# Logit columns of an attention layer turned by VectorE instead of TensorE, and the last half of the output summed by TensorE in PSUM

## The chip, the cores and the metric

The kernel runs on one core of a Trainium2 chip. The metric is the device time of one execution in microseconds (us), the median of several runs. Of the core's engines four compute: PE (TensorE, matrix products into PSUM; its weight loads are shown as PEld), DVE (VectorE), ACT (ScalarE) and POOL (GpSimd). SP (SyncE) only issues transfers. Each engine runs its own instructions in the order in which they were emitted, and waits for other engines and for transfers by semaphores.

## The reference

There are 16 batches of N = 1024 nodes with D = 128 values each, and one symmetric 0/1 matrix `adj` of 1024 x 1024 with ones on its diagonal. All is fp32.

```python
h = x @ Wo;  u1 = h @ a1;  u2 = h @ a2           # layer 0: attention
e = u1[:, idx1] + u2[:, idx2]                    # pair logits, a 1024 x 1024 matrix
e = where(e >= 0, e, 0.1 * e)
att = softmax(where(adj > 0, e, -9e15), axis=1)
x = layernorm(x + att @ h + x @ Ws)
h = x                                            # layer 1: five gated steps
for _ in range(5):
    m = adj @ h;  av = concat([m, m])
    g = h @ u3.T + b_u3
    z = sigmoid(av @ w3.T + b3 + g);  r = sigmoid(av @ w4.T + b4 + g)
    hv = tanh(av @ w5.T + b5 + (r * h) @ u5.T + b_u5)
    h = (1 - z) * h + z * hv
out = layernorm(x + h)
```

Because of how `idx1` and `idx2` run, the logit of row i and column j is, in the first 512 rows, (u1 + u2) of node 2i or 2i + 1, by the half of the columns that j lies in; in the last 512 rows it is u1[2j] + u2[2j + 1] (modulo 1024), the same for all rows. The softmax runs over the rows. So a batch needs three columns of 1024 numbers: u1, u2, and the exponential of the clipped leaky ReLU of u1 + u2.

## The kernel before

**The plan.** Every operation of the whole kernel, is put into a `Plan` (L53 on): engine, expected length in ns, a rank, a function that emits it, the tiles that it reads and writes, and a lag until its result is taken as seen. `order` (L79) plays this through like a clockwork: whenever an engine is free, it takes the ready operation of the lowest rank for which tile buffers are free. The order of starts found that way is the order in which the program is emitted. So nothing is written out by hand; lengths, lags and ranks set the order on every queue. Ranks come from a table `D` (one entry per kind of operation), a due time per batch and step (`rank_of` L321, `rank0` L324; 10 units from one pair of batches to the next), and `NUDGE`, small amounts added for single batches and steps. An `add` under the engine "DMA" emits nothing: it only tells the plan when a load is expected to land (`lands` L366).

**The start.** `early_loads` (L348) issues the first loads on SP's and ACT's queues: x of batch 0 in two halves, the row of attention weights, `Wo`, the halves of `adj`. `late_loads` (L376) issues the step weights, u3, u5 and five rows of biases in one block. PE meanwhile runs fillers: two products of `fill_` and 48 operations `idle_` of two transposes each (L439), of rank 9000, which are taken when nothing else is ready. `ahead` (L466) computes x(Ws + 1) for four later batches and puts it to DRAM. `own_weights` (L489) turns the biases into columns and adds the two halves of w3, w4, w5, since both halves of av are m.

**Layer 0**, `layer0(b)` (L654), for each batch: products ph (L686) give h and the two logit numbers of each node; hx (L696) takes them out of PSUM; `u_` (L701) and `p_` (L709) put three columns of 8 numbers per partition into `u`: two logit columns and an exponential. These must get from node-in-partition order into two other forms: `pb`, the exponentials of all nodes in every partition, and `uu`, pairs of logits in another arrangement of nodes. For batches 2 to 15 PE transposes u, 128 x 24, into PSUM (L725), DVE copies it (L730), SP stores it to `ud` in DRAM (L735), and loads it again as a broadcast (`pb`, L742) and, with two transfers of single numbers, as `uu` (L750). Batches 0 and 1 do without DRAM: 0 has its spreading products from the weights (L763), 1 multiplies each column by the unit matrix (L795) and ACT copies (L804); both have pair products of 4 columns (L813). Then come `t_` (L829: the sum `seen`, leaky ReLU), `q_`, the sums over neighbours `z_` (L849), the factor rz, the blocks hi (L901, ACT) and lo (L907, DVE), products `po` (L644), and a layernorm.

**Layer 1** works on pairs of batches, whose five steps interleave with those of the pair before and with layer 0 of later batches. `messages` (L1089) computes adj @ h by products of halves with seven instead of eight products per batch, using sums of quarters of adj (`sums_of_adj`, L512); operands pass through DRAM (X, loaded as G) where they must be turned. Steps listed as plain multiply directly (blocks `blk_h`, hi on ACT L632 and lo on DVE L636). `gates` (L1211), per half e of 512 nodes: pu (L1228), gate products (L1238), tanh for r and z (L1241), r times h (L1248), products for hv (L1254, L1255), tanh (L1260), and three DVE operations: less (L1263), times (L1266) and h (L1269). With tanh(x/2) in place of the sigmoid, h + 0.5 (z + 1)(hv - h) is the new h. Even batches keep h with the other sign.

**The end.** `end` (L1284), for the last two batches: x is loaded again from `yd` (L1291), h is transposed by PE (L594), DVE adds both (L1301), and `layernorm` (L535) takes statistics (DVE L540, L542), a power (POOL L546, L547) and scales (ACT L561, or for the very last half DVE L567, "short"). The output leaves on SP and ACT (L1318, L1320). The last step is 4, the last half (b, s, e) = (15, 4, 1).

## Time and profile before

| | us |
|---|---|
| median of 3 runs (lowest, highest) | 1450.19 (1449.73, 1451.22) |
| profiled execution | 1449.74 |
| its span, first to last instruction | 1447.6 |
| PE, DVE, ACT, POOL busy in the span | 1432.1, 1161.1, 895.3, 196.9 |

The mean granted clock of PE was 0.997; 1.00 in each stretch of the first 100 us, and 0.81 in the last 22.6 us, where PE is idle in the end. Transfers move 120 GB/s on average, and 340 GB/s in the first 25 us.

A group's row gives the line, engine, operation, output and inputs, how many, busy time and the mean of one in ns, then the idle time before it and what ended it. The timeline's rows give start, length, engine, line and operation; instructions of one line that follow each other are put together (x16), and square brackets give an idle time and its releaser. The queue of SP is SPq. Two matmul rows overlap, since a row holds the latency of a product and the next starts before it has ended: what a product costs a busy PE is the distance of two starts.

### The profile page before, as it was taken

How to read it: one execution, taken by the hardware profiler on the slowest of the kernel's cores; microseconds unless marked ns; L12 is line 12 of the kernel's file. 1: busy time of each engine (PE TensorE's matmuls, PEld its weight loads, DVE VectorE, ACT ScalarE, POOL GpSimd, SP SyncE). 2: the span in 40 equal slices, each digit the busy share in tenths (PEclk: the TensorE clock that was granted, in tenths of full speed). 3: DMA queues.
4: the chain of work that ended last, by engine and by line, in shares of the span. 5: the costliest groups of instructions: out<-in, count | busy, mean ns of one | idle time of the engine just before them, and what ended most of it. 6: DMA issues, size and time to landing. Idle time of an engine off the chain costs nothing.

```text
span 1447.6 us, 17700 instructions
## 1 busy us (share of the span) xinstructions
PE 1432.1 (99%) x4995; PEld 898.2 (62%) x4995; DVE 1161.1 (80%) x2748; ACT 895.3 (62%) x1790; POOL 196.9 (14%) x327
## 2 busy tenths in 40 slices
PE   9999999999999999999999999999999999999996
PEld 7666656666666666656566665666666665656563
DVE  6897888979888899968888788887987977764635
ACT  5666555666665666666746667567574676563644
POOL 1231000022111120111201011011110122000302
PEclk9999999999999999999999999999999999999998
DMA  8235234573335643454343643456424364222111
GB/s 280 96 105 180 61 94 131 153 211 110 108 105 146 188 111 109 122 163 117 102 124 111 189 104 93 116 161 175 107 77 109 96 203 124 80 59 68 50 44 31
DMA packets 187902, 174.14 MB, mean 120 GB/s; under 512 B 34238, under 2 KB 137236, under 8 KB 187796
## 3 DMA queue, kind: packets, MB, share of 16 engines
q1 hardware_dynamic: 181490, 154.71, 37.7%
q0 software_dynamic: 5888, 17.83, 3.7%
q8 instruction: 41, 0.67, 0.2%
q14 instruction: 65, 0.53, 0.1%
q10 hardware_dynamic: 418, 0.39, 0.1%
HBM read 95.61 MB, written 77.24 MB: 119 GB/s over the span
## 4 chain that ended last, share of the span: by engine, by line
PE 95%; DVE 2%; POOL 1%; DMA 0%; ACT 0%; issue 0%; SPq 0%; POOLq 0%; DVEq 0%; ACTq 0%
PE ps_acc_a L644 17%; PE ps_g_r L1238 9%; PE gz L1238 9%; PE ps_g_v L1254 9%; PE ps_g_v L1255 9%; PE ps_g_r L1228 9%; PE ps_acc_c L644 9%; PE ps_acc_po L644 7%; PE ps_acc L644 6%; PE gz L644 4%; PE ps_g_ph L686 2%; PE ps_idle L441 1%; PE ps_acc_po L978 1%; PE ps_t L594 1%; PE ps_acc_px L964 1%; PE ps_ahead L477 0%
## 5 line engine op out<-in xcount | busy, mean ns | idle before, releaser
L1254 PE MATMUL ps_g_v<-m,wm 128*128 128x512 f32 x320 | 163.5, 592 | 0.0
L1255 PE MATMUL ps_g_v<-r,u5h 128*128 128x512 f32 x320 | 163.4, 592 | 0.0
L1238 PE MATMUL ps_g_r<-m,wm 128*128 128x512 f32 x320 | 159.8, 593 | 0.1
L1238 PE MATMUL gz<-m,wm 128*128 128x512 f32 x320 | 159.4, 592 | 0.0
L1248 DVE SCALAR_TENSOR_TENSOR r<-r,hT 128x512 f32<-128x512 f32 x160 | 109.2, 687 | 61.9 <-ACT r L1241 60.6
L1263 DVE TENSOR_TENSOR hv<-hv,hT 128x512 f32<-128x512 f32 x160 | 109.6, 685 | 59.2 <-ACT hv L1260 58.4
L1228 PE MATMUL ps_g_r<-hT,u 128*128 128x512 f32 x320 | 154.2, 592 | 0.0
L644 PE MATMUL ps_acc_a<-tab,blk_s 128*128 128x512 f32 x544 | 150.4, 418 | 0.0
L1241 ACT ACTIVATE r<-ps_g_r,bh 128x512 f32<-128x512 f32 x160 | 109.6, 686 | 65.0 <-PE ps_g_r L1238 62.0
L644 PE MATMUL ps_acc_po<-adj,blk 128*128 128x512 f32 x512 | 143.7, 425 | 0.0
L1231 ACT COPY gz<-ps_g_r 128x512 f32<-128x512 f32 x160 | 91.1, 572 | 63.0 <-PE ps_g_r L1228 61.6
L644 PEld LDWEIGHTS ps_acc_a<-tab,blk_s 128*128 128x128 f32 x544 | 101.1, 188 | 36.3 <-issue 10.3
L1241 ACT ACTIVATE z<-gz,bh 128x512 f32<-128x512 f32 x160 | 109.7, 687 | 15.4 <-PE gz L1238 15.2
L644 PEld LDWEIGHTS ps_acc_po<-adj,blk 128*128 128x128 f32 x512 | 95.9, 188 | 37.1 <-issue 15.3
L1269 DVE SCALAR_TENSOR_TENSOR hT<-hv,hT 128x512 f32<-128x512 f32 x160 | 108.5, 679 | 2.3
L1266 DVE SCALAR_TENSOR_TENSOR hv<-z,hv 128x512 f32<-128x512 f32 x160 | 108.8, 680 | 0.8
L1255 PEld LDWEIGHTS ps_g_v<-r,u5h 128*128 128x128 f32 x320 | 60.7, 190 | 76.6 <-issue 62.0
L1238 PEld LDWEIGHTS gz<-m,wm 128*128 128x128 f32 x320 | 60.7, 190 | 73.9 <-issue 73.2
L644 PE MATMUL ps_acc<-adj,blk_h 128*128 128x512 f32 x384 | 100.8, 413 | 0.5 <-DVE us L730 0.5
L636 DVE TENSOR_TENSOR blk_s<-G,blk_s 128x512 fp32r<-128x512 f32 x136 | 91.8, 682 | 11.3 <-ACT blk_s L632 10.8
L602 DVE STREAM_TRANSPOSE T<-hT 128x512 f32<-128x512 f32 x138 | 96.2, 702 | 0.8 <-DMA D_y<-T_y 0.2
L1254 PEld LDWEIGHTS ps_g_v<-m,wm 128*128 128x128 f32 x320 | 60.3, 190 | 56.4 <-issue 48.9
(193 smaller groups left out, 2518.2 us busy)
## 6 DMA issues: line engine op xcount, KB each, us to landing
G<-X SPq DMA_DIRECT2D x140, 256.0 KB
X<-T SPq DMA_DIRECT2D x552, 64.0 KB
yd<-y POOLq DMA_DIRECT2D x32, 256.0 KB, 3.3
D_y<-T_y SPq DMA_DIRECT2D x112, 64.0 KB
F_y<-D_y SPq DMA_DIRECT2D x28, 256.0 KB
X<-y SPq DMA_DIRECT2D x28, 256.0 KB
D_b<-T_b SPq DMA_DIRECT2D x112, 64.0 KB
F_b<-D_b SPq DMA_DIRECT2D x28, 256.0 KB
```

Source lines behind the costliest of these rows:

```text
L602: nc.vector.transpose(T(t).rearrange("p (b c i) -> p b c i", b=4, c=4), turned(src()))
L636: lambda: nc.vector.tensor_tensor(half(1), src(), half(0), ALU.subtract),
L644: nc.tensor.matmul(T(bank), T(blk)[:, k, c, :], right(c), start=(first and i == 0), stop=(last and i == len(terms) - 1), skip_group_check= ...
L1228: nc.tensor.matmul(T(pr), u3, h(), start=True, stop=True)
L1238: nc.tensor.matmul(T(p_), wm[:, j, :], T(m), start=False, stop=True, skip_group_check=True)
L1241: nc.scalar.activation(T(t), T(p_), AF.Tanh, bias=bh[:, j : j + 1], scale=0.5 * sg)
L1248: lambda r=r, h=h: nc.vector.scalar_tensor_tensor(T(r), T(r), 1.0, h(), ALU.add, ALU.mult),
L1254: nc.tensor.matmul(T(pv), wm[:, 2, :], T(m), start=True, stop=False)
L1255: nc.tensor.matmul(T(pv), u5h, T(r), start=False, stop=True)
L1263: nc.vector.tensor_tensor(T(hv), T(hv), h(), ALU.subtract)
L1266: nc.vector.scalar_tensor_tensor(T(hv), T(z), 1.0, T(hv), ALU.add, ALU.mult)
L1269: nc.vector.scalar_tensor_tensor(h(), T(hv), 0.5, h(), ALU.mult, ALU.add)
```

## The change

1. **Attention row.** It is loaded first on ACT's queue, ahead of half of x.
2. **Logit columns.** `u` gets four columns instead of three (the first is the last column of h, which nothing reads), so that it is 128 x 32. DVE transposes it in blocks of 32 x 32 within SBUF; SP stores the result to `ud` as 128 rows of 32 numbers. PE's transpose and DVE's copy from PSUM go. Batch 1 takes this way too: its spreading and pair products and ACT's copies go, and it waits for transfers through DRAM.
3. **Transfers of the start.** The planned landings are set anew; `late_loads` become single operations that the plan puts behind batch 1's `uu` load (key `b1`), and so do the x loads from batch 4 on and those of the last batch of `ahead`. `layer0(1)` is planned ahead of the rest.
4. **The very last half.** A new function `finish` replaces less, times, h, transposes and addition of (15, 4, 1). The hv products and tanh come in two pieces of 256 columns. With old = (z - 1) h, PE sums x, -0.5 old and 0.5 (z + 1) hv, each against a unit matrix (turning the last two), into two PSUM banks, from which the layernorm reads. The epsilon of its variance is added by DVE. All of batch 15 is now scaled by DVE, and batch 14's last scale by ACT waits for the last tanh.
5. **Ranks.** `D` and `NUDGE` are set anew; `NUDGE` has new kinds of keys for halves and for operations of the end.

```diff
-NUDGE = {(3, 2): -0.6, (3, 3): 0.75, (0, 1): -0.45,
...
+NUDGE = {(3, 2): 1.8, (3, 3): 0.95, (0, 1): 0.15,
...
+(15, 4, 0): 0.15, (15, 2): 0.3, ('add', 14, 1): 0.15, ('add', 15, 0): -0.1, ('ln', 14, 1): -0.6, ('ln', 15, 0): -1.2, 15: 0.05, ('add', 14, 0): -0.6}
...
-        D = dict(m=-0.05, pu=1.4, u=0.95, pr=0.75, pz=0.85, r=0.45, pv=1.05, z=1.3, hv=0.5, h=1.2, tr=2.35, o=6.35, ln=2.5, out=4.4, l1=-9, l2=-7, l3=-2.2, l4=-4.5, l5=-7.25)
...
+        D = dict(m=-0.05, pu=-0.1, u=3.45, pr=0.75, pz=0.85, r=1.45, pv=0.05, z=2.8, hv=0.5, h=-0.8, tr=2.35, o=6.35, ln=2.5, out=4.4, l1=-9.2, l2=-9, l3=-2.2, l4=-3.5, l5=-7.25)
...
         def early_loads():
             nc.sync.dma_start(T(x0)[:, HALF:N], x_t[0][:, HALF:N])
+            nc.scalar.dma_start(T(ws)[0:1, P : 3 * P], att_w.rearrange("k o -> o k"))
             nc.scalar.dma_start(T(x0)[:, 0:HALF], x_t[0][:, 0:HALF])
-            nc.scalar.dma_start(T(ws)[0:1, P : 3 * P], att_w.rearrange("k o -> o k"))
...
-        lands(4650, [(x0, 0), (x0, 1), (ws, "att")])
-        lands(650, [(("wo",), 0)])
-        for ns, k, e in ((2000, 0, 0), (1400, 0, 1), (1400, 1, 0), (1400, 1, 1), (1600, 2, 0), (1400, 2, 1), (1400, 3, 0), (1400, 3, 1)):
+        lands(4700, [(x0, 0), (x0, 1), (ws, "att"), (("wo",), 0)])
+        for ns, k, e in ((1500, 0, 1), (3100, 0, 0), (300, 1, 1), (1900, 1, 0), (1800, 2, 1), (1000, 2, 0), (1700, 3, 1), (1500, 3, 0)):
...
-        lands(1400, [(("xt", 1), 0), (("xt", 1), 1)])
...
+        lands(500, [(("xt", 1), 0), (("xt", 1), 1)])
         def late_loads():
+            def load(t, what, to, by):
+                sp(450, -7.9, lambda: nc.sync.dma_start(to(), by), reads=[(("b1",), 0)], writes=[(t, what)], lag=2600)
             for j, w in enumerate((w3_t, w4_t, w5_t)):
-                nc.sync.dma_start(
...
+                load(
...
                 )
-            nc.sync.dma_start(u3, u3_t)
-            nc.sync.dma_start(u5, u5_t)
+            load(("uw",), 0, lambda: u3, u3_t)
+            load(("uw",), 1, lambda: u5, u5_t)
             for j, v in enumerate((w3_b, w4_b, w5_b, u3_b, u5_b)):
-                nc.sync.dma_start(T(ws)[j : j + 1, 3 * P : 4 * P], v.rearrange("(o p) -> o p", o=1))
...
+                load(ws, ("b", j), lambda j=j: T(ws)[j : j + 1, 3 * P : 4 * P], v.rearrange("(o p) -> o p", o=1))
...
-                    sp(450, -91, lambda x=x, b=b, hs=hs: nc.sync.dma_start(T(x), x_t[b][:, hs]), writes=[(x, "sent")], lag=0)
+                    sp(450, -91, lambda x=x, b=b, hs=hs: nc.sync.dma_start(T(x), x_t[b][:, hs]), reads=[(("b1",), 0)] if b == AHEAD[-1] else [], writes=[(x, "sent")], lag=0)
...
+            if split:
+                def half(i):
+                    for j in range(2 * i, 2 * i + 2):
+                        nc.vector.bn_stats(T(stats)[:, j, :], src(j))
+                    for j in range(2 * i, 2 * i + 2):
+                        nc.vector.bn_aggr(T(mv)[:, j, :], T(stats)[:, j, :])
+                    if i:
+                        nc.vector.tensor_scalar(T(rstd)[:, 0, :], T(mv)[:, :, 1], EPS, None, ALU.add)
+                dve(570, rank, lambda: half(0), reads=after[0:1], writes=[(stats, 0), (mv, "a")])
+                dve(730, rank, lambda: half(1), reads=[*after[1:2], (mv, "a")], writes=[(stats, 1), (mv, 0), (rstd, "e")])
...
-                sp(450, rank, lambda: nc.sync.dma_start(T(xt), x_t[b]), writes=[(xt, 0), (xt, 1)], lag=3500)
+                sp(450, rank, lambda: nc.sync.dma_start(T(xt), x_t[b]), reads=[(("b1",), 0)], writes=[(xt, 0), (xt, 1)], lag=3500)
...
-                nc.vector.tensor_copy(w[:, 0:2, :], h[:, :, P : P + 2].rearrange("p c t -> p t c"))
+                nc.vector.tensor_copy(w[:, 0:3, :], h[:, :, P - 1 : P + 2].rearrange("p c t -> p t c"))
...
-            if b >= 2:
-                put = ("ps", "t", b, "u")
-                pe(
-                    120,
+            if b >= 1:
+                dve(
+                    110,
                     rank,
-                    lambda: nc.tensor.transpose(T(put)[0 : 3 * NC, 0:P], T(u).rearrange("p t c -> p (t c)"), ident),
-                    reads=[(u, 0), (u, 1), (("ident",), 0)],
-                    writes=[(put, 0)],
-                )
-                dve(
-                    280, rank, lambda: nc.vector.tensor_copy(T(us), T(put)[0 : 3 * NC, 0:P]), reads=[(put, 0)], writes=[(us, 0)]
+                    lambda: nc.vector.transpose(T(us), T(u).rearrange("p t c -> p (t c)")),
+                    reads=[(u, 0), (u, 1)],
+                    writes=[(us, 0)],
                 )
                 sp(
                     450,
                     rank,
-                    lambda: nc.sync.dma_start(T(ud).rearrange("t (c p) -> (t c) p", p=P), T(us)),
+                    lambda: nc.sync.dma_start(T(ud).rearrange("t (c k i) -> k (t c) i", k=4, i=32), T(us)),
                     reads=[(us, 0)],
                     writes=[(ud, 0)],
                 )
                 sp(
                     450,
                     rank,
-                    lambda: nc.sync.dma_start(T(pb), T(ud)[2:3, :].to_broadcast([P, N])),
+                    lambda: nc.sync.dma_start(T(pb), T(ud)[3:4, :].to_broadcast([P, N])),
                     reads=[(ud, 0)],
                     writes=[(pb, 0), (pb, 1)],
                     lag=3000,
...
                 def uu_():
                     for w in range(2):
-                        nc.sync.dma_start(T(uu)[:, w, :], T(ud)[w].rearrange("(c p two) -> two p c", p=P, two=2)[w])
-                sp(950, rank, uu_, reads=[(ud, 0)], writes=[(uu, 0)], lag=3000)
+                        nc.sync.dma_start(T(uu)[:, w, :], T(ud)[w + 1].rearrange("(c p two) -> two p c", p=P, two=2)[w])
+                sp(950, rank, uu_, reads=[(ud, 0)], writes=[(uu, 0), *([(("b1",), 0)] if b == 1 else [])], lag=3000)
...
-                        def spread_(e=e, pp=pp):
-                            for j in range(4):
-                                c = 4 * e + j
-                                nc.tensor.matmul(
-                                    T(pp)[:, j * P : (j + 1) * P],
-                                    T(u)[:, 2, c : c + 1].to_broadcast([P, P]),
-                                    ident,
-                                    start=True,
-                                    stop=True,
-                                )
-                        def pb_(e=e, pp=pp):
-                            nc.scalar.copy(T(pb)[:, e * HALF : (e + 1) * HALF], T(pp))
-                        pe(920, rank, spread_, reads=[(u, 0), (u, 1), (("ident",), 0)], writes=[(pp, 0)])
-                        act(A, rank, pb_, reads=[(pp, 0)], writes=[(pb, e)])
...
+        def finish(b, s, rank, sg, m, r, z, hv, pv, h):
+            old, units = ("T", b, s, "old"), ("look", "units")
+            o, yd = ("y0", b, "o", 1), ("yd", b, 1)
+            plus, minus = T(units)[:, 0:P], T(units)[:, P : 2 * P]
+            def units_():
+                nc.vector.tensor_scalar(plus, ident, 0.5, None, ALU.mult)
+                nc.vector.tensor_scalar(minus, ident, -0.5, None, ALU.mult)
+            def old_():
+                nc.vector.scalar_tensor_tensor(T(old), T(z), 1.0, h(), ALU.subtract, ALU.mult)
+            dve(260, rank - 0.6, units_, reads=[(("ident",), 0), (m, 0)], writes=[(units, 0)])
+            sp(
+                450,
+                rank,
+                lambda: nc.sync.dma_start(T(o).rearrange("p c d -> p (c d)"), T(yd)),
+                reads=[(yd, 0), (("m", b, s, 0), 0)],
+                writes=[(o, "y")],
+                lag=2300,
+            )
+            dve(V, rank + D["hv"] - 0.3 + NUDGE.get(("old", b), 0), old_, reads=[(z, 1), (("hT", b), 1)], writes=[(old, 0)])
+            for f in range(2):
+                cs = slice(2 * P * f, 2 * P * (f + 1))
+                t = ("ps", "t", b, s, 1, f)
+                def pv_(cs=cs):
+                    nc.tensor.matmul(T(pv)[:, cs], wm[:, 2, :], T(m)[:, cs], start=True, stop=False)
+                    nc.tensor.matmul(T(pv)[:, cs], u5h, T(r)[:, cs], start=False, stop=True)
+                def hv_(cs=cs):
+                    nc.scalar.activation(T(hv)[:, cs], T(pv)[:, cs], AF.Tanh, bias=b5 if sg > 0 else nb5, scale=1.0)
+                def times_(cs=cs):
+                    nc.vector.scalar_tensor_tensor(T(hv)[:, cs], T(z)[:, cs], 1.0, T(hv)[:, cs], ALU.add, ALU.mult)
+                def y_(t=t, f=f):
+                    for j in range(2):
+                        nc.tensor.matmul(
+                            T(t)[:, j * P : (j + 1) * P], ident, T(o)[:, 2 * f + j, :], start=j == 0, stop=False, skip_group_check=True
+                        )
+                def add_(t=t, f=f, what=None, unit=None, last=False):
+                    for j in range(2):
+                        c = 2 * f + j
+                        nc.tensor.matmul(
+                            T(t)[:, j * P : (j + 1) * P],
+                            T(what)[:, c * P : (c + 1) * P],
+                            unit,
+                            start=False,
+                            stop=last,
+                            skip_group_check=True,
+                        )
+                part = [(pv, 0)] if f else []
+                pe(F, rank + D["pv"], pv_, reads=[*part, (m, 0), (r, 2), (("wm",), 0), (("uw",), 0)], writes=[(pv, f)])
+                pe(F / 2, rank + D["tr"], y_, reads=[(o, "y"), (("ident",), 0), (pv, f)], writes=[(t, 0)])
+                pe(F / 2, rank + D["tr"], lambda add_=add_: add_(what=old, unit=minus), reads=[(old, 0), (units, 0)], writes=[(t, 0)])
+                act(A / 2 + 80, rank + D["hv"], hv_, reads=[(pv, f), (("wm",), 0)], writes=[(hv, ("h", f))])
+                dve(V / 2 + 60, rank + D["hv"], times_, reads=[(hv, ("h", f)), (z, 1)], writes=[(hv, ("t", f))])
+                pe(
+                    F / 2,
+                    rank + D["tr"],
+                    lambda add_=add_: add_(what=hv, unit=plus, last=True),
...
+                rank = rank_of(b, s) + (0.8 if (b, s, e) == (B - 1, STEPS - 1, 1) else 0) + NUDGE.get((b, s, e), 0)
...
+                if (b, s, e) == (B - 1, STEPS - 1, 1):
+                    finish(b, s, rank, sg, m, r, z, hv, pv, h)
+                    continue
...
-            later = [(("hv", B - 1, STEPS - 1, g), 0)] if b == B - 2 else []
-            layernorm(("o", b), g, rank + D["ln"], (o, "raw"), src, dst, (o, 0), sign(b), b == B - 1 and g == 1, later)
+            later = [(("hv", B - 1, STEPS - 1, 1), ("h", 1))] if b == B - 2 else []
+            layernorm(("o", b), g, rank + D["ln"] + NUDGE.get(("ln", b, g), 0), after, src, dst, (o, 0), sign(b), b == B - 1, later, split=very)
...
-        ahead()
         for c in range(NC):
             adj_tables(c)
+        dve(270, -8, self_, reads=[(boot, "ws"), (("ident",), 0)], writes=[(("wsi",), 0)])
+        layer0(1)
+        late_loads()
+        ahead()
         for b in range(B):
-            layer0(b)
+            if b != 1:
+                layer0(b)
```

## Prediction

> **What bounds the kernel now.** I read the page first: its share of busy time and the chain that ended last.
>
> ```profile
> PE 1432.1 (99%) x4995; PEld 898.2 (62%) x4995; DVE 1161.1 (80%) x2748; ACT 895.3 (62%) x1790; POOL 196.9 (14%) x327
> ...
> PE 95%; DVE 2%; POOL 1%; DMA 0%; ACT 0%; issue 0%; SPq 0%; POOLq 0%; DVEq 0%; ACTq 0%
> ```
>
> TensorE is the bound: 95% of the last chain. To see whether it has hidden gaps I added up what each of its instructions takes when the next follows at once (512 columns 0.429 us by the starts of neighbouring products, 128 columns 0.109) and set this against elapsed time: from 0 to 50 us elapsed is 2.5 us longer than the sum, from 50 to 100 0.35, then nothing until the last gates end at about 1432.9. So PE work removed anywhere shortens the run, unless another engine paces that stretch; and after 1432.9 a serial tail counts for itself. The second view is the table of stretches (busy time of PE, weight loads, DVE, ACT, POOL; granted clock; DMA share; GB/s):
>
> ```profile
> 0.00:25.00 25.00, 23.58 (x155) 18.55 (x156) 13.26 (x56) 13.75 (x40) 3.98 (x13) 1.00 0.99 340
> 25.00:50.00 25.00, 24.50 (x122) 17.47 (x122) 21.13 (x79) 16.90 (x43) 5.65 (x10) 1.00 0.45 153
> 50.00:75.00 25.00, 25.00 (x102) 16.82 (x101) 22.71 (x85) 13.79 (x40) 5.11 (x3) 1.00 0.23 71
> ```
>
> The start is full of transfers until 25 us, and then DVE is nearly as full as PE (21.1, 22.7 of 25). There a PE saving might not survive. Third, the timeline around the logit columns:
>
> ```profile
> 26.14 1.95 PE L795 MATMUL ps_p<-ident,u 128*128 128x128 f32 x16
> ...
> 28.02 0.42 PE L813 MATMUL ps_pairs<-u,ident 128*64 128x4 f32 x8
> ...
> 44.60 0.31 SPq L735 DMA_DIRECT2D ud<-us  x1
> 44.72 4.26 PE L644 MATMUL ps_acc<-adj,blk_h 128*128 128x512 f32 x16 [0.46 <-DVE us L730]
> ...
> 47.16 1.35 SPq L750 DMA_DIRECT2D uu<-ud  x2
> ...
> 52.64 0.16 DVE L829 TENSOR_TENSOR seen<-uu 128x4 f32<-128x4 f32 x1 [1.25 <-DMA uu<-ud]
> ```
>
> **The change part by part.** *The attention row first.* In the trace's landing events the row lands at 4.44, the x halves at 4.19 and 4.36, `wo` at 4.62. The first product that uses the row starts later, behind fillers:
>
> ```profile
> 4.99 2.05 PE L441 MATMUL ps_idle<-ident 128*128 128x128 f32 x16
> 6.97 0.69 PE L414 MATMUL ps_g_w<-T_ws,ones 1*128 1x256 f32 x2
> ```
>
> Those 16 transposes stand ahead of it in the changed order too. Worth 0; the cover is the 2.05 us of fillers.
>
> *PE work removed by the columns.*
>
> ```profile
> L725 PE MATMUL ps_t_u<-ident,u 128*24 128x128 f32 x14 | 3.8, 272 | 0.0
> L795 PE MATMUL ps_p<-ident,u 128*128 128x128 f32 x16 | 1.9, 275 | 0.0
> ```
>
> The 272 ns of a row is its latency; its place in the stream is 0.108 (next start minus own start). So 14 x 0.108 = 1.51 for batches 2 to 15; batch 1's 16 spreading passes 28.02 - 26.14 = 1.88 (1.79 at 0.112 each, the value I take) and its pairs 28.36 - 28.02 = 0.34. Sum 3.64, on the bound. In exchange DVE copies (0.273, 14 times) become 15 transposes of 128x32 within SBUF. The nearest rows are 0.702 for a transpose of 128x512 and 0.16 for a 128x4 operation: 0.16 to 0.28, I take 0.18. ACT loses two copies of 0.59 for batch 1.
>
> *The wait this adds.* Batch 1 gets its columns through DRAM: `ud`, then `pb` and two `uu`. Walking the changed order with durations of the trace: `ud` leaves at about 26, `pb` at 27.4, `uu` at 27.9 and 28.4, landing at 31.4 to 32.5 (a `pb` took 4.84 from issue to landing at 46.69, and the two `uu` behind it 4.58 and 4.70; alone they took 2.0 to 2.1). DVE reaches its `seen` addition at 32.5 to 33.1: just in time, bounds 0 and 1.2 (the wait at 52.64). Behind that addition on DVE stand batch 0's layernorm statistics, behind those POOL's power, ACT's scale, `blk_h`, and PE's first products of messages. Batch 2's addition is wanted at 49.2 with `uu` landing at 48.5 to 49.5: 0 to 0.3. Four late weight loads and five bias rows are now issued on SP's queue behind batch 1's `uu`, one by one at about 0.22 to 0.45 each; the last lands near 40 and PE wants the biases at 41.4, so 0 while that margin of 1.4 lasts.
>
> [...] `ud` was 24 rows of 512 B and landed in 1.33 us (44.60 to 45.93); it becomes 128 rows of 128 B. [...] But the `uu` loads fetch their numbers four bytes at a time and still land in 2.0 to 2.1 when alone. That row bounds the far smaller number of 128 B pieces from above: 1.3 to 2.1, I take 1.5. The measured row weighs more, so I keep 0.3 of extra stall at the start, with ends 0 and 2.
>
> *Ranks anew.* The order and the number of fillers (96 x 0.109 + 4 x 0.85 = 13.9 us) stay as they were in amount; the order of layer 0 shifts. Walking PE: the second message product of batch 0 starts at about 42.5 instead of 45.22, a lead of 2.3 to 2.7; then stalls of 0.75 and 0.4 where `blk_h` comes from DVE, against 0.63 + 0.27 before. That difference is the 0.25 to 0.3 just named; nothing else falls due late until 62. In the steps, the shortest turn from a gate to the products that use it goes from 18.1 to 18.3 us in one class and from 25.0 to 20.4 in another, and the last pair's gates come bunched (about 14 us without message products between), with 0.2 to 0.3 us of margin for the transposes of h. I find no stall, so 0, with ends -0.5 (a stall of the start goes) and +8.
>
> *The tail.* Time t counts from the last batch's first r gate in step 4 (1425.58 before).
>
> ```profile
> 1432.03 1.02 PE L1255 MATMUL ps_g_v<-r,u5h 128*128 128x512 f32 x2
> 1433.50 0.67 ACT L1260 ACTIVATE hv<-ps_g_v,b 128x512 f32<-128x512 f32 x1
> 1434.20 0.69 DVE L1263 TENSOR_TENSOR hv<-hv,hT 128x512 f32<-128x512 f32 x1
> ...
> 1439.53 0.36 DVE L542 BATCH_NORM_AGGREGATE mv_o<-stats_o 128x2 f32<-128x6 f32 x4
> 1440.24 0.23 POOL L546 TENSOR_SCALAR rstd_o<-mv_o 128x4 f32<-128x4 f32 x1
> 1440.55 1.04 POOL L547 TENSOR_TENSOR rstd_o<-rstd_o,mhalf 128x4 f32<-128x4 f32 x1
> 1441.62 1.12 DVE L567 TENSOR_SCALAR y_o<-y_o,mv_o,rstd_o 128x128 f32<-128x128 f32 x4 [1.73 <-POOL rstd_o L547]
> ```
>
> Before: the gates' last piece is through at t = 7.3, tanh starts at 7.92, DVE does less, times, h (3 x 0.7), waits for transposes, adds, takes statistics: aggregates end at 14.3, power at 16.0, scale at 17.16. The change lets tanh start at once (the 0.27 behind ACT's scale goes) and takes less, h and the addition of this half, 2.1 us, off DVE; it adds there `old` (0.69), two unit matrices (0.3, filled in earlier), the epsilon (0.15) and the scale of the other half (1.1, was ACT's). Twelve 128-column products are added and four dropped, in time when PE is otherwise idle. My walk of the new order: aggregates and epsilon end at 13.1; but POOL's power of the first half runs 12.7 to 13.74, so the last one 13.77 to 14.81; DVE, after the first half's scale (13.78 to 14.9), does the last scale 14.92 to 16.05. Gain 17.16 - 16.05 = 1.1; ends 0 (DVE's turn falls badly once: the scale of the first half comes first and the last waits 1.1 for it) and 2.0 (no wait for POOL). The statistics now read PSUM. [...] The rows say 284 ns from `ps_t_y` against 278 from SBUF: 0.02. [...]
>
> **Sum.** The profiled execution took 1449.74 (span 1447.6, 2.1 around it); the median is 1450.19, 0.45 above. 1449.74 - 3.64 - 1.1 + 0.3 = 1445.3; with 0.45, 1445.75: I predict 1445.8.
>
> **Rivals.** *The start is paced by DVE and by transfers.* For it: DVE's 21 to 23 of 25, the wait of 1.25 for `uu`, batch 1's margin of nothing. Then the PE work removed before 45 us (1.79 + 0.34 + 0.11) turns into stalls, and what is left is 13 x 0.108 = 1.4 and the tail: 1450.2 - 1.4 - 1.1 = 1447.7. Against: the walk finds a lead of over 2 us still at 51.5. *The tail keeps its length.* The chain goes round by DVE and POOL anyway; 1450.2 - 3.64 + 0.3 = 1446.9, inside the likeliest one's range. *Slower: messages fall late in the steps.* ACT waits for the G tiles loaded from DRAM already now:
>
> ```profile
> ACT blk_x L632 <- DMA G<-X: 26.2, 23, 3.6
> ```
>
> That is 23 waits, the longest 3.6, all behind PE work today. The turn that shrinks from 25.0 to 20.4 could bring them to PE. Each pair of batches has such turns; the mechanism decides once the stalls exceed 4.4 + 2.9 = 7.3 us, for instance 2 us in four of the eight pairs. That gives 1445.8 + 8 = 1453.8. Against it: 18.1 was short enough before without a stall. Partly so, at 4 us, it gives 1449.8, no change. *The change doesn't do what it says:* the transposes are gone from PE in the built order, so for the columns this is out; for the attention row it is the likeliest case, worth 0.
>
> **How the numbers follow.** A measurement of this kernel can tell about 0.2%, 2.9 us. Likeliest case (with the tail's rival in it) 0.66, 1444.2 to 1447.2 from the tail's 0 to 2 and the start's 0 to 2, partly against each other; paced start 0.15, 1446.8 to 1448.4; partly late 0.08, 1448 to 1452; slower 0.11, from 1453.1 on. Faster is under 1447.3: nearly all of the first (0.65) and half of the second (0.07), 0.72; within 0.2%: 0.01 of the first, 0.08 of the second, 0.08 of the third, 0.17; slower 0.11. The range that leaves out 2 in 10 cuts the slower case and half of the partly late one above (0.15), and 0.05 below, where a stall of the start also goes: 1443.9 to 1449.8.
>
> **What would show it.** No PE row of 128*24 remains and PE instructions in the first 50 us fall; PE stays gapless from 100 us on; the second message product starts near 42.5; DVE's wait for `uu` of batch 1 stays under 1 us; the wait of PE for `blk_h` stays under 1.5; the time from that r gate to the last scale is 16.0. It is wrong if PE waits for ACT or DVE in a stretch between 100 and 1420 us, or if the lead at 42.5 is gone by 62.

## The result

The changed kernel takes 1446.98 us (median of 10 runs, 1445.74 to 1448.08), the kernel before 1450.16 (1449.62 to 1451.22): a ratio of 0.9977, 95% interval 0.9967 to 0.9986, 3.2 us faster. 1445.8 had been predicted, 4.4 faster. The profiled execution took 1447.51, its span is 1445.7; it stands 0.5 above its median, the one of before 0.4 below its own.

The page, shares of busy time and the chain that ended last:

```profile
PE 1431.1 (99%) x4981; PEld 898.2 (62%) x4981; DVE 1161.5 (80%) x2755; ACT 890.4 (62%) x1785; POOL 199.9 (14%) x324
...
PE 96%; DMA 1%; DVE 1%; ACT 1%; SPq 0%; issue 0%; POOL 0%; DVEq 0%; ACTq 0%; POOLq 0%
```

TensorE is still the bound. DMA and ACT now have 1% each of the chain, where the page of before rounds both to 0%: among the long pieces of the chain there are now four transfers with 19.7 us in all (loads of `uu`, `look`, G and `pb`), before there were two with 7.0. The stretches of the first 75 us (PE, weight loads, DVE, ACT, POOL busy; granted clock; DMA share; GB/s):

```profile
0.00:25.00 25.00, 23.58 (x150) 18.52 (x151) 12.48 (x52) 13.01 (x37) 3.98 (x13) 1.00 0.93 321
25.00:50.00 25.00, 24.48 (x112) 17.70 (x110) 20.06 (x80) 17.18 (x46) 6.12 (x10) 1.00 0.72 210
50.00:75.00 25.00, 24.18 (x99) 16.30 (x98) 23.42 (x86) 16.57 (x49) 5.09 (x9) 1.00 0.20 61
```

Transfers have moved from the first 25 us into the next (0.45 to 0.72 of the DMA engines, 153 to 210 GB/s), and from 50 to 75 us PE is short of work for 0.8 us, where it was full. The waits of PE (us in total, times, longest), first two of before, then those of the changed kernel:

```profile
PE ps_t L594 <- DVE hT L1269: 2.8, 2, 1.5
PE ps_acc L644 <- DVE us L730: 0.5, 1, 0.5
```

```profile
PE gz_fill L448 <- POOL ident masks.py:199: 1.4, 1, 1.4
PE ps_g_r L1288 <- ACT m L1174: 0.8, 1, 0.8
PE ps_acc_po L660 <- DVE blk L899: 0.8, 1, 0.8
PE ps_acc_a L660 <- ACT m L1174: 0.5, 1, 0.5
PE ps_acc L660 <- ACT hT L1066: 0.5, 1, 0.5
```

The second, third and fourth are new; the fifth stands where PE waited for DVE's copy of the columns, and is as long. The 2.8 us of waiting for `hT` in the tail are gone. The tail's timeline:

```profile
1424.77 1.02 PE L1298 MATMUL ps_g_r<-m,wm 128*128 128x512 f32 x2
...
1432.29 0.84 ACT L1234 ACTIVATE hv<-ps_g_v,b 128x256 f32<-128x256 f32 x2 [1.04 <-PE ps_g_v L1231]
...
1437.32 2.02 POOL L550 TENSOR_TENSOR rstd_o<-rstd_o,mhalf 128x4 f32<-128x4 f32 x2
...
1439.42 1.36 DVE L570 TENSOR_SCALAR y_o<-ps_t,mv_o,rstd_o 128x128 f32<-128x128 f32 x4
```

From the last batch's first r gate (1424.77) to the end of the last scale (1439.42 + 1.36 = 1440.78) it is 16.01 us; it was 17.16.

A ledger of the two profiled spans, PE's elapsed time against the sum of what its instructions take when they follow at once:

| | before | after | difference |
|---|---|---|---|
| PE work removed ahead of the tail | | | -3.64 |
| lost from 0 to 50 us, of it by the clock's start (below) | 2.50 | 2.58, of it 0.9 more | +0.08 |
| lost from 50 to 100 us | 0.36 | 1.15 | +0.8 |
| lost from 100 to 1425 us | -1.19 | 0.5 | +1.7 |
| tail, r gate to last scale | 17.16 | 16.01 | -1.15 |
| sum | | | -2.2 |

The measured difference of the spans is 1.9. (A negative loss means that the unit times are a little large; only differences count.) Without the clock's 0.9 the sum is -3.1, close to the difference of the medians, -3.2; how the clock began in the executions without a profile is not known. The row from 100 to 1425 us rests on one execution each. Counted the same way in the other traces, the loss there lies 0 to 1.7 us above that of before in the four whose steps have the old order of work, and 0.7 to 2.7 in the six that have the new one; the means differ by 1.3.

### The profile page after: what moved, and what is told of

The parts are those of the page before. It is cut to its first block, busy times and chain, and to the rows that moved or that the text cites. A ratio compares the mean times of both kernels' runs of the same rounds, so it can differ in the third digit from the quotient of the medians.

```text
span 1445.7 us, 17588 instructions
## 1 busy us (share of the span) xinstructions
PE 1431.1 (99%) x4981; PEld 898.2 (62%) x4981; DVE 1161.5 (80%) x2755; ACT 890.4 (62%) x1785; POOL 199.9 (14%) x324
## 4 chain that ended last, share of the span: by engine, by line
PE 96%; DMA 1%; DVE 1%; ACT 1%; SPq 0%; issue 0%; POOL 0%; DVEq 0%; ACTq 0%; POOLq 0%
PE ps_acc_a L660 17%; PE ps_g_r L1298 10%; PE gz L1298 9%; PE ps_g_r L1288 9%; PE ps_g_v L1314 9%; PE ps_g_v L1315 9%; PE ps_acc_c L660 9%; PE ps_acc_po L660 8%; PE ps_acc L660 5%; PE gz L660 4%; PE ps_g_ph L702 2%; PE ps_idle L444 1%; PE ps_acc_po L970 1%; PE ps_t L610 1%; PE ps_acc_px L956 1%; PE ps_ahead L479 0%
## 5 line engine op out<-in xcount | busy, mean ns | idle before, releaser
L660 PE MATMUL ps_acc_a<-tab,blk_s 128*128 128x512 f32 x544 | 160.1, 436 | 0.0
L1288 PE MATMUL ps_g_r<-hT,u 128*128 128x512 f32 x320 | 157.9, 592 | 0.8 <-ACT m L1174 0.8
L549 POOL TENSOR_SCALAR rstd_y<-mv_y 128x4 f32<-128x4 f32 x32 | 15.3, 478 | 641.6 <-DVE mv_y L544 586.6
L1323 ACT ACTIVATE hv<-ps_g_v,nb 128x512 f32<-128x512 f32 x80 | 54.9, 686 | 70.8 <-PE ps_g_v L1315 68.3
```

What stands on the lines that cost most here:

```text
L660: nc.tensor.matmul(T(bank), T(blk)[:, k, c, :], right(c), start=(first and i == 0), stop=(last and i == len(terms) - 1), skip_group_check= ...
L1288: nc.tensor.matmul(T(pr), u3, h(), start=True, stop=True)
```

## The experiments

Each was timed in five rounds beside the kernel before on its own chip; the changed kernel stood at a ratio of 0.9977 both times that it was run, and a variant is compared with it by the difference of the ratios (0.001 is 1.45 us). The interval of a ratio is about 0.0009 to each side, so that of a difference of two is some 0.0013, or 1.8 us.

**The changed kernel once more.** No edit.

> The changed kernel once more, beside the three variants that follow. All theories: about 3.2 us under the kernel before. What is asked of its trace is where PE loses time. In the first trace of the changed kernel the fillers reached full rate (0.109 us from start to start) only at 7.1 us, against 5.4 in the trace before, and PE waited 0.8 near 52, 0.7 near 404 and 1.0 near 544 us. If the late full rate belongs to the change, it is at 7.1 again; if it is chance of an execution, it moves. If the waits near 404 and 544 come from the order, they are there again within some tenths; if from the transfers of one execution, they move or go.

1447.47 us, ratio 0.9977 (0.9969 to 0.9986). The waits of PE in its trace:

```profile
PE ps_g_r L1288 <- ACT m L1174: 0.8, 1, 0.8
PE ps_acc_po L660 <- DVE blk L899: 0.7, 1, 0.7
PE ps_acc L660 <- ACT hT L1066: 0.5, 1, 0.5
```

The wait near 544 us and the one near 52 are there again: they come from the order of work. The one near 404 is not: it belonged to that execution. Instead this execution lost some 0.5 us in each of the stretches of 25 us from 800 and from 1000, where the first had lost nothing. The fillers' full rate came late once more, at 6.96 us. By the expectation that would speak for the change; the further traces decide against it (last section).

**The tail, taken out and put in alone.**

```diff
 # in the changed kernel; the layernorm and the end go back too
-                if (b, s, e) == (B - 1, STEPS - 1, 1):
-                    finish(b, s, rank, sg, m, r, z, hv, pv, h)
-                    continue
...
```

> The changed kernel with the last half done as before (less, times, h, transposes, addition; scale of its first half by ACT). My theory, that the tail counts for itself: 1.1 us slower than the changed kernel, from the last batch's first r gate to the last scale about 17.2 us instead of 16.0. The rival, that the tail goes round by DVE and POOL anyway: 0, and the same 16 to 16.5 us.

1449.12 us, ratio 0.9992 (0.9983 to 1.0): 2.2 us slower by the ratios, 1.65 by the medians. From that r gate (1425.07) to the last scale:

```profile
1440.03 1.04 POOL L550 TENSOR_TENSOR rstd_o<-rstd_o,mhalf 128x4 f32<-128x4 f32 x1
1441.10 1.12 DVE L570 TENSOR_SCALAR y_o<-y_o,mv_o,rstd_o 128x128 f32<-128x128 f32 x4 [1.73 <-POOL rstd_o L550]
```

1441.10 + 1.12 - 1425.07 = 17.15, where the changed kernel has 16.01. Put alone into the kernel before:

```diff
 # in the kernel before: finish(), the split layernorm and the new end(), and of the ranks
+('add', 14, 1): 0.15, ('add', 15, 0): -0.1, ('ln', 14, 1): -0.6, ('ln', 15, 0): -1.2, ('add', 14, 0): -0.6
```

> The kernel before with the new last half alone (with the new amounts for its additions and layernorms, the other ranks as before). My theory: 1.1 us faster than the kernel before. The rival, that the tail goes round by DVE and POOL: 0.

1449.05 us, ratio 0.9990 (0.9981 to 0.9999): 1.5 faster, and 16.01 from gate to scale. So the tail is worth 1.15 us in each trace where it is exchanged, and in all 14 traces it takes 17.15 to 17.16 us in the old form and 16.01 to 16.02 in the new one. The rival, that it goes round by DVE and POOL anyway, falls. What the medians show beyond 1.15 lies within the interval.

**The attention row.**

```diff
             nc.sync.dma_start(T(x0)[:, HALF:N], x_t[0][:, HALF:N])
-            nc.scalar.dma_start(T(ws)[0:1, P : 3 * P], att_w.rearrange("k o -> o k"))
             nc.scalar.dma_start(T(x0)[:, 0:HALF], x_t[0][:, 0:HALF])
+            nc.scalar.dma_start(T(ws)[0:1, P : 3 * P], att_w.rearrange("k o -> o k"))
```

> The changed kernel with the attention row second on ACT's queue, as before. All theories: 0, since the product that needs it stands behind fillers until 7 us and the row landed at 4.4.

1446.97 us, ratio 0.9977 (0.9968 to 0.9986): nothing. In the changed kernel the row lands at 1.99 us instead of 4.44, and the product that needs it starts at 7.86.

**Parts undone, planned anew.** Three variants undo a part in the source and let the plan find a new order.

```diff
 # batch 1 on PE
-            if b >= 1:
+            if b >= 2:
... (the spreading products, pairs and ACT's copies come back)
```

> The changed kernel with batch 1's columns made on PE as before (16 spreading passes, its pairs, two copies by ACT); batches 2 to 15 stay with DVE. The late loads wait for its pair product instead. My theory, PE sets the pace of the start: 2.1 us slower than the changed kernel (1.79 + 0.34). The rival, the start is paced by DVE and by transfers: 0, or up to 0.8 faster since the wait for the columns in DRAM goes.

```diff
 # PE turns the columns
-                    lambda: nc.vector.transpose(T(us), T(u).rearrange("p t c -> p (t c)")),
+                    lambda: nc.tensor.transpose(T(put)[0 : 4 * NC, 0:P], T(u).rearrange("p t c -> p (t c)"), ident),
...
+                    280, rank, lambda: nc.vector.tensor_copy(T(us), T(put)[0 : 4 * NC, 0:P]), reads=[(put, 0)], writes=[(us, 0)]
```

> The changed kernel with the columns of batches 1 to 15 turned by PE into PSUM and copied by DVE, and stored in rows of 512 B; all else as changed, batch 1 through DRAM too. My theory: 15 x 0.108 = 1.6 us slower than the changed kernel. The rival, in which the start has slack on PE: 1.4 (13 of them). If storing rows of 128 B were dear, the first columns would land later in the changed kernel than here: its store took 1.3 us in the kernel before; I expect 1.5 against 1.3.

```diff
 # the ranks of the kernel before: its NUDGE and D
-NUDGE = {(3, 2): 1.8, (3, 3): 0.95, (0, 1): 0.15,
+NUDGE = {(3, 2): -0.6, (3, 3): 0.75, (0, 1): -0.45,
```

> The changed kernel with the ranks (D and NUDGE) of the kernel before. If the new ranks brought the waits near 404 and 544 us and cost their 1.7 us, this is 1.7 faster than the changed kernel. If they are what lets the removed PE work count at the start, it is slower, by up to 3. My theory, which gave them 0: within 0.5 of the changed kernel.

They took 1479.38, 1472.28 and 1453.63 us: 32, 25 and 5 to 6 more than the changed kernel, where 2.1, 1.6 and at most 0.5 had been expected. No sum of instructions explains that. In the first, the waits of PE begin with

```profile
PE ps_acc_c L660 <- ACT blk_s L648: 11.3, 1, 11.3
```

one wait from 652 to 664 us, and on SP's queue between 600 and 665 us one issue stood for 10.2 us behind a scale of a layer-0 batch:

```profile
SPq L1074 <- ACT y L564: 10.7, 2, 10.2
```

As I read it, the plan has laid layer 0 of a later batch and messages of an earlier one into the same time; that reading was not tested. So these three measure an order found for another amount of work, not the part that was undone.

The long waits of PE cost twice here. In the first variant TensorE's granted clock falls to 0.50 during two of them and stays there for a while: for 6.8 and 13.7 us, with waits of 4.4 and 11.3; by the distances of starts (512 columns 0.853 us instead of 0.429) the two cost about 3 us each on top of the waits. Over all 14 traces, every wait of PE of 3.2 us or more comes with half the clock, of two waits of 2.5 us one does, and ahead of the tail no shorter one.

With the old ranks the changed work is even slower than the kernel before (ratio 1.0014, 1.0005 to 1.0023). In its trace the steps lose 6.5 us more than in the changed kernel; 2.5 of it is one wait near 828 us, with half the clock for 3.4 us behind it. So the parts together, planned anew, need the new ranks. The tail alone, above, needed only the new amounts of the end, and the turning of batches 2 to 15, below, needs none.

A fourth was to hold back no loads.

> The changed kernel with the late loads in one block and no load held back for batch 1's columns, as before; all else as changed. If the held-back loads are what keeps batch 1's columns in time, these land 2 to 3 us later here, behind the other transfers of the first 30 us, and the kernel is 1 to 2 us slower than the changed one. If that order does nothing, 0.

1485.95 us. The edit missed its aim: it issued the late weight loads also ahead of everything, so that half of x of batch 0 and `wo` landed at 12.1 and 12.9 us and VectorE waited 13.0 us for `wo`. It says nothing of held-back loads, so what holding them back is worth stays open. Its longest wait of PE, 10.9 us near 656 us, is for the same blocks as the 11.3 us above; the rest of the loss was not taken apart.

**Parts exchanged in a fixed order.** Therefore the plan is made from the unchanged list of operations, and only what an operation emits is exchanged; all other instructions keep their place on every engine.

```diff
 # in the kernel before: columns of batches 2 to 15 (u with four columns, rows of 128 B)
-                    lambda: nc.tensor.transpose(T(put)[0 : 3 * NC, 0:P], T(u).rearrange("p t c -> p (t c)"), ident),
+                    lambda: None,
...
-                    280, rank, lambda: nc.vector.tensor_copy(T(us), T(put)[0 : 3 * NC, 0:P]), reads=[(put, 0)], writes=[(us, 0)]
+                    280, rank, lambda: nc.vector.transpose(T(us), T(u).rearrange("p t c -> p (t c)")), reads=[(put, 0)], writes=[(us, 0)]
```

> The kernel before in its own order of work, instruction for instruction; alone the columns of batches 2 to 15 are turned by DVE in SBUF and stored in rows of 128 B, and PE's 14 transposes are gone. My theory, PE is the bound: 14 x 0.108 = 1.5 us faster than the kernel before. The rival, that the order of work fits only its own content (as the variants planned anew were 25 to 38 us slower): slower, or no faster.

1448.66 us, ratio 0.9982 (0.9973 to 0.9991): 2.1 to 2.6 faster for 1.5 expected, with PE's sum of unit times down by 1.53. What is beyond it lies within the interval. As the order is the same, this pair shows what the smaller pieces cost the store of the columns. By the landing events of the 14 stores, its median from issue to landing is 1.94 us with rows of 128 B and 1.32 with rows of 512 B; for batch 2 it is 2.77 and 1.33.

```diff
 # and batch 1 too, where its spreading products stood
                         def spread_(e=e):
                             if e:
                                 return
+                            nc.vector.transpose(T(us), T(u).rearrange("p t c -> p (t c)"))
+                            nc.sync.dma_start(T(ud).rearrange("t (c k i) -> k (t c) i", k=4, i=32), T(us))
+                            nc.sync.dma_start(T(pb), T(ud)[3:4, :].to_broadcast([P, N]))
+                            for k in range(2):
+                                nc.sync.dma_start(T(uu)[:, k, :], T(ud)[k + 1].rearrange("(c p two) -> two p c", p=P, two=2)[k])
```

> As the one before it, and batch 1's columns through DRAM too, issued where its spreading products stood; all other work in the order of the kernel before. If PE sets the pace of the start: 3.6 us faster than the kernel before. If batch 1's transfers arrive late where no loads are held back for them: 1.5 faster or less, with a wait of DVE for these columns of 2 us or more behind which PE stands.

1456.87 us, ratio 1.0040 (1.0026 to 1.0053): 5.8 slower than the kernel before, though PE has 3.6 us less to do. The timeline where DVE wants the columns:

```profile
29.21 0.64 SPq L796 DMA_DIRECT2D ud<-us  x1
...
37.66 0.16 DVE L829 TENSOR_TENSOR seen<-uu 128x4 f32<-128x4 f32 x1 [9.02 <-DMA uu<-ud]
...
39.33 0.79 PE L644 MATMUL ps_acc_po<-adj,blk 128*128 128x512 f32 x1 [6.83 <-DVE blk L907]
```

The columns were turned at 26.59, but their store left SP at 29.21, behind bias and x loads, took 3.75 us to land, and `uu` landed at 37.57. DVE stood at its addition for 9.0 us and started nothing else in that time, and PE stood for 6.8. PE came back at half the clock, as two stretches show (columns as above; the granted clock is the third number from the end):

```profile
34.70:39.30 4.60, 0.00 (x0) 0.00 (x0) 1.54 (x7) 0.84 (x4) 0.00 (x0) 0.50 0.68 195
39.30:44.90 5.60, 5.57 (x7) 2.39 (x8) 5.53 (x19) 1.87 (x4) 0.00 (x0) 0.50 0.24 95
```

Six of its products start 0.79 to 0.85 us apart instead of 0.43, which costs about 2.8 us more. The wait and the half clock make 9.7; with 3.6 us less work and without the 0.5 that PE waited here before, 5.6 are left of it, close to the 5.8. In the changed kernel the store leaves at 25.81, the last `uu` lands at 32.77, and DVE takes it up at 33.72 without waiting for it. This is the late wait that the expectation named. In the changed kernel it is hidden: there the columns are turned 1.0 us sooner and their store leaves at once, ahead of the bias and x loads. Which of the held-back loads, the new landings and the new ranks does that, this run doesn't separate.

```diff
 # in the changed kernel: PE turns, DVE copies, rows of 512 B
-                    lambda: nc.vector.transpose(T(us), T(u).rearrange("p t c -> p (t c)")),
+                    nc.tensor.transpose(T(put)[0 : 4 * NC, 0:P], T(u).rearrange("p t c -> p (t c)"), ident)
+                    nc.vector.tensor_copy(T(us), T(put)[0 : 4 * NC, 0:P])
...
-                    lambda: nc.sync.dma_start(T(ud).rearrange("t (c k i) -> k (t c) i", k=4, i=32), T(us)),
+                    lambda: nc.sync.dma_start(T(ud).rearrange("t (c p) -> (t c) p", p=P), T(us)),
```

> The changed kernel in its own order of work; alone the columns of batches 1 to 15 are turned by PE into PSUM and copied by DVE, and stored in rows of 512 B. My theory: 15 x 0.108 = 1.6 us slower than the changed kernel (so 1.6 faster than the kernel before), up to 2.5 with the waits of PE for the exponential ahead of it. If the slowness of this variant planned anew (25 us over the changed kernel) came from PE's transposes themselves, it is slow here too; if from the new order, it is not.

1450.43 us, ratio 0.9996 (0.9987 to 1.0005): 2.8 slower than the changed kernel, for 1.6 to 2.5. PE's sum is up by 1.64; two waits of PE that end at DVE's copies, 0.4 each, add to it, and the interval holds the rest.

```profile
PE ps_g_b L412 <- DVE us L740: 0.4, 1, 0.4
PE ps_g_r L1293 <- DVE us L740: 0.4, 1, 0.4
```

The same exchange that cost 25 us when planned anew costs 2.8 in a fixed order: 22 went with the new order, about 3 of them by half the clock near 660 us.

```diff
 # in the changed kernel: batch 1 alone, at the place of its turn
-                    lambda: nc.vector.transpose(T(us), T(u).rearrange("p t c -> p (t c)")),
+                        for c in range(4 * e, 4 * e + 4):
+                            nc.tensor.matmul(T(pp)[:, (c - 4 * e) * P : (c - 4 * e + 1) * P], T(u)[:, 3, c : c + 1].to_broadcast([P, P]), ident, start=True, stop=True)
+                        nc.scalar.copy(T(pb)[:, e * HALF : (e + 1) * HALF], T(pp))
... (its pairs; no store and no loads for batch 1)
```

> The changed kernel in its own order of work; alone batch 1's columns are made on PE as before (16 passes, its pairs, two copies by ACT), without transfers. My theory: 2.1 us slower than the changed kernel. The rival, the start is paced by DVE and by transfers: 0 to 0.8 faster. Planned anew this variant took 32 us more than the changed kernel; if that was the order, it is gone here.

1449.92 us, ratio 0.9995 (0.9986 to 1.0004): 2.6 slower than the changed kernel, for 2.1. The first message products, in the changed kernel and in this variant:

```profile
43.09 3.99 PE L660 MATMUL ps_acc<-adj,blk_h 128*128 128x512 f32 x16 [0.52 <-ACT hT L1066]
```

```profile
44.37 4.00 PE L660 MATMUL ps_acc<-adj,blk_h 128*128 128x512 f32 x16 [0.52 <-ACT hT L1093]
```

From the start of the product for the attention row (7.86 and 6.82), which takes the clock's start out, these are 35.23 and 37.55 us: 2.3 later for 2.13 of work. So the rival, that the start is paced by DVE and transfers and batch 1's products cost nothing, falls for this order of work. Not all of the 2.6 need be PE work, though: batch 2's store took 4.67 us in this trace (2.60 in the changed kernel), and PE's wait at batch 2's block is 1.7 us instead of 0.8.

**The single parts don't add up.** Undone one by one, tail, turning and batch 1 cost 2.2, 2.8 and 2.6 us, 7.6 together, where their work is worth 4.8 by the walk and the whole change brought 3.2. Put alone into the kernel before, tail and turning brought 1.5 and 2.1 to 2.6, as much as the whole change; whether they bring that together was not run. With an interval of 1.3 us for a single ratio and 1.8 for a difference, and with waits that move with every exchange, these are signs and sizes, not shares of the 3.2. It stays open whether batch 1's way through DRAM, with the loads and ranks that it came with, gains anything in the end.

## Why the prediction was right, and where it was off

**Attention row, 0:** right, with the row back it is the same.

**PE work, -3.64:** right. By the unit times the work is gone, and in a fixed order 1.5 to 1.6 us of turning measured 2.1 to 2.8 and 2.1 us of batch 1's products 2.6, each within its interval. The rival of a paced start is out: the second message product began at 43.42 instead of 45.22, and without the 0.9 us by which the clock started later that is the 42.5 of the walk.

**The columns' transfers:** for batch 1 the walk held ("just in time", `uu` at 31.4 to 32.5 and wanted at 32.5 to 33.1; measured 32.6 to 32.8 and 33.7). For batch 2 a term was mis-sized: `uu` was to land at 48.5 to 49.5, wanted at 49.2, a stall of 0 to 0.3. It landed at 50.55 and 51.37.

```profile
49.75 0.69 DVE L841 SCALAR_TENSOR_TENSOR junk<-adj,pb 128x512 f32<-128x512 f32 x1 [1.55 <-DMA pb<-ud]
...
51.46 0.16 DVE L821 TENSOR_TENSOR seen<-uu 128x4 f32<-128x4 f32 x1 [1.01 <-DMA uu<-ud]
...
53.15 1.90 PE L660 MATMUL ps_acc_po<-adj,blk 128*128 128x512 f32 x7 [0.82 <-DVE blk L899]
```

DVE waits for `pb`, then for `uu`; PE waits behind DVE's lo block, and 0.8 us are lost from 50 to 100. The store of the columns had been put at 1.5 us, with an upper bound of 2.1; it took 2.03 for batch 1 and 2.60 for batch 2, against 1.33 before. With rows of 512 B in the same order it was 1.40 and 2.69. So for batch 1 the smaller pieces cost 0.6, as in the median of the fixed-order pair above. For batch 2 the store is slow with either size of piece in this order, and in the order of before only with the small one (2.77 against 1.33). I had given the traffic around it no price, and the bound, taken from loads that ran alone, didn't hold. That batch 2 pays for the loads held back for batch 1, which now move between 25 and 50 us, is likely from the DMA share there (0.45 to 0.72), but no run shows it.

**Ranks, 0 with -0.5 to +8:** the likeliest value was off. A gain and a loss hide behind it: the stalls of the start before 50 us became 0.85 smaller beside the clock, not larger by 0.3; but the steps lose 1.7 more than before. By its own signs the prediction fails here: PE was to stay gapless from 100 us on, and it was to be wrong if PE waits for ACT between 100 and 1420 us. The waits come to 1.4 of the 1.7. They have two forms. One is that of the rival of late messages, far below the 8 us at which it was priced, near 404 us in the profiled execution:

```profile
403.20 0.62 ACT L648 CAST blk_x<-G 128x512 fp32r<-128x512 f32 x1 [2.50 <-DMA G<-X]
403.73 0.59 ACT L1174 ACTIVATE m<-ps_acc_a 128x512 f32<-128x512 f32 x1
...
404.37 0.96 PE L660 MATMUL ps_acc_a<-tab,blk_x 128*128 128x512 f32 x3 [0.54 <-ACT m L1174]
```

ACT stands at the cast for a G tile, and PE waits for the copy of a finished product behind it. It comes and goes between executions. The other was in no rival. It is there in all six traces with the new order of work, near 544 us, and in none with the old one: a scale of an output batch of 1.65 us on ACT's queue stands ahead of such a copy.

```profile
542.89 1.65 ACT L564 ACTIVATE o<-o,rstd_o 128x128 f32<-128x128 f32 x4
...
544.45 0.57 ACT L1174 ACTIVATE m<-ps_acc_a 128x512 f32<-128x512 f32 x1
...
545.08 1.12 PE L1288 MATMUL ps_g_r<-hT,u 128*128 128x512 f32 x2 [0.83 <-ACT m L1174]
```

The walk looked at turns from gate to products and at the last pair; it didn't look at what ACT has ahead of the copies that release PE. How much of the 1.7 the new ranks cost is not settled: a trace in the old order (`f_before_turn`) loses as much over the one of before, and over all traces the orders differ by 1.3.

**Tail, -1.1:** right in mechanism and size, 16.01 for a walk of 16.05. Inside it two small errors cancel: POOL's two powers ended 0.24 sooner, and the last scale, which reads PSUM, took 1.36 instead of 1.13. The groups of the two scales:

```profile
L570 DVE TENSOR_SCALAR y_o<-ps_t,mv_o,rstd_o 128x128 f32<-128x128 f32 x4 | 1.4, 402 | 0.0
L570 DVE TENSOR_SCALAR y_o<-y_o,mv_o,rstd_o 128x128 f32<-128x128 f32 x4 | 1.1, 342 | 0.7 <-POOL rstd_o L550 0.7
```

In this trace the scale that reads PSUM (`ps_t`) takes 402 ns, the one that reads SBUF 342; I had walked both with the time of the row from SBUF. The statistics stayed alike, as walked (280 from PSUM, 272 to 283 from SBUF).

**Sum.** -3.64 - 0.05 (the first 100 us without the clock: -0.85 + 0.8) + 1.7 - 1.15 = -3.1 for -4.4 predicted. The measured 1446.98 lies in the likeliest case's own range (to 1447.2), but that is in part luck: the range was made of the start and the tail, which came out as walked, and the shortfall of 1.3 comes from the steps, for which the likeliest case had 0.

## What to carry to other kernels

Where one engine is dense, count removed work by the distance of starts, and walk the serial tail instruction by instruction: the tail came out within 0.1 us, the removed work within the interval of the runs. The slack of moved work has to be checked on the engines that release the bound one, with their waits for transfers (ACT's 2.50 us for a G tile here) and long operations ahead of short copies (a scale of 1.65 ahead of a copy of 0.57), in every stage and not only next to the edit. And where a planner sets the order, undo a part by exchanging what an operation emits in a fixed order: the same part cost 2.6 to 2.8 us so, and 25 to 32 with a new plan. Where a wait of the bound engine comes near 3 us (2.5 to 3.2 here), look at the clock behind it too.

## What had not been expected

TensorE's fillers begin at half their later rate: the first takes 1.01 us and the next ones 0.853 (512 columns, 0.429 later), and the transposes after them 0.213 us from start to start until they change to 0.109. The moment of that change differs between executions: 5.3 us before, 7.1 and 7.0 in the two traces of the changed kernel, and from 4.6 to 7.4 over all 14 traces. It does not go with the change: four traces with the old start have it at 4.6, 5.3, 6.3 and 7.4, ten with the new or a varied one from 4.9 to 7.2. The product for the attention row, which stands behind 16 of them, starts at 6.65 to 8.0 us. The timeline of the changed kernel, for the rows that the prediction showed of before:

```profile
4.99 2.93 PE L444 MATMUL ps_idle<-ident 128*128 128x128 f32 x16
7.86 0.69 PE L417 MATMUL ps_g_w<-T_ws,ones 1*128 1x256 f32 x2
```

2.93 for 2.05: 0.9 us of the difference between the two profiled executions is this, and not the change. A start that moves so could make 1.35 of the 2.3 us by which the changed kernel's runs differ (6.65 to 8.0), though only the profiled ones can be looked into. PE's first filler starts at 1.42 us in both profiled executions, so the change comes 3.9 us behind it before and 5.7 in the changed kernel. The granted clock in the table of stretches reads 1.00 all through it, so the rate has to be read from the distance of starts; this holds for the 1.00 of the first 25 us of the kernel before as well.
